# Eight layers on one core: a quarter of one key transpose moved from VectorE to TensorE, reciprocals moved to GpSimd

## The chip, the cores and the metric

The kernel runs on one core of one Trainium2 chip. The metric is device microseconds of one execution, from the first to the last instruction and what lies around it. Before the change three runs gave a median of 3522.67 us (3521.52 to 3526.77).

A core has five engines that run side by side, each with its own queue of instructions: TensorE (PE in the profile, with its weight loads as PEld), VectorE (DVE), ScalarE (ACT), GpSimd (POOL) and SyncE (SP), which starts DMAs here. They wait for one another by semaphores.

## The reference, cut to what matters

A stack of eight layers works on one sequence of 2048 tokens of 128 values, each as `x = x + f(layernorm(x))`: four attentions (L0 to L3) and four feed-forward layers. The attention of L2 is cheap here. Those of L0, L1 and L3 have 16 heads of 64 values and differ in mask and bias:

```python
# L0 (full attention; L1 is causal; L3 has a region mask and a bias per query and head)
Q = jnp.einsum('btd,hkd->bthk', x, W_Q) + b_Q
K = jnp.einsum('btd,hkd->bthk', x, W_K) + b_K
V = jnp.einsum('btd,hkd->bthk', x, W_V) + b_V
scores = jnp.einsum('bqhk,bshk->bhqs', Q, K) / jnp.sqrt(jnp.asarray(d_head, x.dtype))
attn = jax.nn.softmax(scores, axis=-1)
out_h = jnp.einsum('bhqs,bshk->bqhk', attn, V)
return jnp.einsum('bqhk,hdk->bqd', out_h, W_O) + b_O
```

L0 and L3 look at all 2048 keys for every query. The kernel calls these the layers that are not causal; the change calls them full.

## The kernel before, in words

**The order of the work.** Nothing is issued where it is written. Every piece of work is a `Step` (L92) with an engine, an estimated time `us`, a key (tick, place) and lists of steps and buffers that it needs. `run` (L119) is a list scheduler in Python: again and again it takes the engine that can start a step earliest, prefers the lowest key among what is ready, and emits that step's instructions. Each engine then executes its instructions in that order. So the estimates set the order of every queue, though not a single wait. `Ring` and `Held` (L78, L86) are the buffers: a step that takes a buffer waits until the users of the one that it replaces are done.

**One pair, eight groups.** An attention runs pair by pair of heads (8 pairs). `Pair` projects the keys, queries and values of its two heads from the normalised, transposed x: `projected` (L385, eight matmuls of 512 columns a pair), `valued` (L405, four times four matmuls of 128 columns). A `Group` (L420) is 256 queries of a pair, as eight strips of 32 queries. There are 8 groups to a pair, 64 to a layer.

**One group of a full layer**, by step, with its line:

- `score` (L458, matmuls L481): for each of eight strips and both heads, four matmuls of 64x512, one for each quarter of the partitions: the score tile of a strip and a head is 128 x 512. Partition 32c + q holds query q, column 32b + k holds key k of block 4b + c. Two strips are glued to one step, so a group has four. In the profile a 4-byte matmul stands as two records: 32 to such a step. L3 adds a small mask matmul to each strip and head (`picks`).
- `scan` (L491, DVE): copies a score tile from PSUM to the row buffer e and takes its lowest value on the way: 16 a group, each with a short read of the accumulator.
- `spread_lowest` (L525): GpSimd gathers the lowest values (L537), DVE reduces them (L540), in L3 GpSimd adds the bias (L544), ACT hands the result out (L551). Twice a group, for j = 0 and 1, each four strips.
- `exps` (L559, ACT, L563): 16 a group, in place, with their sums.
- `turn` (L577, DVE, L580): transposes 32x32 blocks of e in place, four strips at a time: four a group, (j, h) from (0, 0) to (1, 1), each 128 x 2048. After it, the partitions of 32-column slice t hold keys 128t to 128t + 127.
- `weigh` (L584, matmuls L595): four steps c = 0 to 3 a group, each 8 matmuls (four t, two heads) of 128x256 with v as weights; head 0 writes partitions 0 to 63 of o, head 1 partitions 64 to 127. A step c = 0 waits for all four turns.
- `sum_up` (L607): 8 tiny matmuls (L614) bring the sums to the queries' partitions, DVE takes their reciprocal (L626).
- `project_out` (L631): ACT copies o (L655), PE multiplies by the output weights (L640), ACT scales by the reciprocals (L650), GpSimd adds to x (L668).

A group's scores stand at ticks 4g to 4g + 3, its turns at 4g + 4 to 4g + 7, its weighing at 4g + 8 to 4g + 11 of the pair: three groups are under way at once, with six row buffers e (two a group), four PSUM banks for scores (`BANKS`), three for all else (`MISC`) and one for o.

Of the kernel before, what the change touches and what calls it, by code (L numbers as in the profile page):

```python
# [13 lines left out]
ALU = mybir.AluOpType  # L14
AX = mybir.AxisListType

P = 128
T = 2048
D = 128
NT = T // P  # L20
H = 16
DH = 64
# [8 lines left out]
Q = 32  # L31
NS = 8
# [26 lines left out]
def network(ctx: ExitStack, tc: tile.TileContext, a: dict, out: bass.AP):  # L59
# [128 lines left out]
    MID, MIXED, PAIRED = Ring(work, "mid4", [P, 512], 4), Ring(work, "mid3", [P, 512], 3), Ring(work, "mid2", [P, 512], 2)  # L188
    LOW, SHIFT = Ring(small, "low", [P, 4, NS], 3), Ring(small, "shift", [P, NS], 3)
    SUMS, SHARES = Ring(small, "sums", [P, 2, NS], 3), Ring(small, "r", [P, 2, 2], 3)  # L190
    OUT, PARTS = Ring(small, "oT", [P, NS * Q], 2), Ring(small, "part", [P, 2, D], 4)
    MEANS, NORMED = Ring(small, "mv", [P, 4, 4], 3, ordered=False), Ring(small, "xn", [P, 4, D], 2, ordered=False)

    def keep(shape, name, dtype=F32):
        return one.tile(list(shape), dtype, tag=name, name=name)
# [27 lines left out]
    make_identity(nc, ident)  # L223
    half_power = keep([P, 4], "half_power")
    nc.gpsimd.memset(half_power, -0.5)
    xT = keep([P, PAD + T], "xT")
    nc.gpsimd.memset(xT[:, 0:PAD], 0.0)

# [136 lines left out]
    class Pair:  # L365
# [19 lines left out]
        def projected(self, add, c, to, which, s, takes):  # L385
            pp, b = Held(MISC), self.layer.biases[which]

            def make():
                nc.tensor.matmul(  # L389
                    pp.t, lhsT=self.w.t[:, which, :], rhs=xT[:, cols(4 * c, 4)], start=True, stop=True  # L390
                )

            def copy():
                part = to.t[:, bass.ts(c, 512)] if which else to.t
                if b is not None:
                    nc.scalar.activation(part, pp.t, AF.Identity, bias=b[:, self.p : self.p + 1], scale=s)
                else:
                    nc.scalar.mul(part, pp.t, s)

            uses = [self.w] if takes else [self.w, to]  # L400
            made = add(PE, 0.62, make, self.layer.ready[c], takes=[pp] + takes, uses=uses)
            self.layer.readers[c].append(made)
            return add(ACT, 0.6, copy, uses=[pp, to])

        def valued(self, add, c):  # L405
            pv, v = Held(MISC), self.v[c]

            def make():
                for i in range(4):
                    nc.tensor.matmul(  # L410
                        pv.t[:, bass.ts(i, P)], lhsT=xT[:, cols(4 * c + i)], rhs=self.w.t[:, 2, :], start=True, stop=True
                    )

            made = add(PE, 0.8, make, self.layer.ready[c], takes=[pv, v], uses=[self.w])
            self.layer.readers[c].append(made)
            self.v_made.append(
                add(ACT, 0.6, lambda: nc.scalar.copy(v.t.rearrange("p t d -> p (t d)"), pv.t), uses=[pv, v])
            )

    class Group:  # L420


        def __init__(self, pair, g, t0, late, t1):
            self.pair, self.g, self.layer = pair, g, pair.layer
            self.narrow = self.width(NS - 1) <= 256
            self.rows = [Held(ROWS)] if self.narrow else [Held(ROWS), Held(ROWS)]
            self.sums, self.o, self.oT = Held(SUMS), Held(SUMMED), Held(OUT)
            self.lows, self.shifts = [Held(LOW) for j in range(2)], [Held(SHIFT) for j in range(2)]
            scanned = [self.score(planner(t0 + k, SCORES), planner(t0 + k, LOWEST), k) for k in range(4)]
            turned = []  # L430
            summed = []
            for j in range(2):
                found = scanned[2 * j] + scanned[2 * j + 1]
                shifted = self.spread_lowest(planner(t0 + 2 + 2 * j, SMALL), planner(t0 + 3 + 2 * j, SMALL), j, found)
                for h in range(2):
                    tick = t0 + 4 + 2 * j + h
                    made = [
                        self.exps(planner(tick, MORE if part else EXPS), j, h, part, shifted) for part in range(2)
                    ]
                    summed += made  # L440
                    turned.append(self.turn(planner(tick + late, TURN), j, h, made))
            shares = self.sum_up(planner(t0 + 8, SMALL), summed)
            n = g // 2 + 1 if self.layer.causal else 4
            weighed = []
            for c in range(n):
                weighed = [self.weigh(planner(t1 + c, WEIGH), c, turned + weighed)]
            self.project_out(t1 + n, weighed, shares)
# [10 lines left out]
        def score(self, add, add_scan, k):  # L458
# [37 lines left out]
            needs = pair.k_made[0 : self.g // 2 + 1 if causal else 4] + [pair.q_made[self.g // 2]]  # L496
            needs = needs + masks if causal or masked else needs
            n = self.width(2 * k)
            us = max(0.25, 0.0019 * n) + (0.1 if causal else 0.07 if masked else 0.0)
            used = [pair.kT, pair.qT[self.g // 2]]  # L500
            second = add(PE, us, lambda: make(2 * k + 1, banks[1]), needs, takes=banks[1], uses=used)
            first = add(PE, us, lambda: make(2 * k, banks[0]), needs, takes=banks[0], uses=used, then=second)
# [56 lines left out]
        def exps(self, add, j, h, part, shifted):  # L559
# [14 lines left out]
            us = 2 * (0.29 + 0.00082 * self.width(4 * j))  # L574
            return add(ACT, us, do, [shifted], takes=[self.sums] if first else [], uses=uses)

        def turn(self, add, j, h, made):  # L577
            def do():
                e = self.e(h)[:, bass.ts(j, 4), 0 : self.width(4 * j)]
                nc.vector.transpose(e, e)  # L580

            return add(DVE, 0.06 + 0.00436 * self.width(4 * j), do, made, uses=self.rows)

        def weigh(self, add, c, turned):  # L584

            last = self.width(4) // Q - 1
            ts = range(4 * c, min(4 * c + 4, last + 1))

            def first(t):
                return 4 if t * Q >= self.width(0) else 0  # L590

            def do():
                for t in ts:
                    for h in range(2):
                        nc.tensor.matmul(  # L595
                            self.o.t[bass.ds(DH * h, DH), first(t) : NS, :],
                            lhsT=self.pair.v[c].t[:, t % 4, bass.ds(DH * h, DH)],
                            rhs=self.e(h)[:, first(t) : NS, bass.ts(t, Q)],
                            start=t == 0,
                            stop=t == last,  # L600
                        )

            us = sum(0.27 if first(t) else 0.487 for t in ts)
            uses = self.rows + [self.pair.v[c]] + ([self.o] if c else [])
            return add(PE, us, do, turned + [self.pair.v_made[c]], takes=[] if c else [self.o], uses=uses)

        def sum_up(self, add, made):  # L607

            ps, r = Held(MISC), Held(SHARES)

            def do():
                for j in range(2):
                    for i in range(4):
                        nc.tensor.matmul(  # L614
                            ps.t[bass.ts(i, Q), bass.ts(j, 2)],
                            lhsT=quarters,
                            rhs=self.sums.t[:, :, 4 * j + i],
                            start=True,
                            stop=True,
                        )  # L620

            add(PE, 0.25, do, made, takes=[ps, r], uses=[self.sums])
            self.shared = add(
                DVE,
                0.17,
                lambda: nc.vector.reciprocal(r.t.rearrange("p j h -> p (j h)"), ps.t[:, 0:4]),  # L626
                uses=[ps, r],
            )
            return r

        def project_out(self, tick, weighed, r):  # L631
# [284 lines left out]
    def feed_forward(add, t0, n, after, full, w1T, b1, func, w2T):  # L916

        hT, made, po = [Held(MID) for f in range(NC)], [], Held(MISC)
        for f in range(0, NC, 2):
            ph = [Held(MISC) for k in range(2)]  # L920

            def make(f=f, ph=ph):
                for k in range(2):
                    nc.tensor.matmul(  # L924
                        ph[k].t[:, 0 : P * n],
                        lhsT=w1T()[:, bass.ts(f + k, P)],
                        rhs=xT[:, cols(t0, n)],
                        start=True,
                        stop=True,
                    )  # L930

            def act(k, ph):
                nc.scalar.activation(
                    hT[k].t[:, 0 : P * n], ph.t[:, 0 : P * n], func, bias=b1[:, k : k + 1]
                )

            add(PE, 0.31 * n, make, after, takes=ph + hT[f : f + 2])
            for k in range(2):
                made.append(
                    add(ACT, wide(P * n), lambda k=k, f=f, ph=ph: act(f + k, ph[k]), uses=[ph[k], hT[f + k]])  # L940
                )
# [90 lines left out]
    def rest(add, t0, n, after, hurry, made):  # L1032
# [31 lines left out]
        for to, part, mu in ((xk, rests[1], mu_k), (xr, rests[0], mu_r)):  # L1064
# [4 lines left out]
        edges.append(kept)  # L1069
        add(  # L1070
            PE,
            0.155 * n,
            lambda: nc.tensor.matmul(pk.t[:, 0:m], lhsT=wkk, rhs=xk.t[:, 0:m], start=True, stop=True),
            mixed[0:1],
            takes=[pk, ka],
# [79 lines left out]
    def features(add, c):  # L1155
# [3 lines left out]
        for j in range(3):  # L1159
# [7 lines left out]
            def act(j=j, n=n, ph=ph):  # L1167
                nc.scalar.activation(hm[j].t[0:n, :], ph.t[0:n, :], AF.Gelu, bias=eb1[0:n, j : j + 1])

            add(PE, 0.62, make, L3.ready[c], takes=[ph, hm[j]])  # L1170
            made.append(add(ACT, 0.6 if j else 1.9, act, uses=[ph, hm[j]]))

        def score():
# [204 lines left out]
```

## Time and profile before

| what | before |
|---|---|
| median of three runs | 3522.67 us |
| profiled execution's own time | 3522.59 us |
| its span, first to last instruction | 3520.9 us |
| mean granted TensorE clock | 0.985 |
| PE busy | 3421.9 us (97%) |
| PEld busy | 1722.5 us (49%) |
| DVE busy | 3281.8 us (93%) |
| ACT busy | 2720.9 us (77%) |
| POOL busy | 774.2 us (22%) |
| L0 attention, steady part | about 30 to 1165 us |
| L1 attention, with the layers around it | about 1165 to 2300 us |
| L3 attention, steady part | about 2300 to 3440 us |

Busy time is the union of an engine's instructions. A matmul's end is modelled, so the durations of PE rows overlap; the distance from the start of a step to the start of the next is the firmer number, and it is used below. The chain of waits follows the work that ended last back from the end, each step to what released it. A group of instructions is shown with its count, its busy time, the mean length of one in ns, and the idle time of its engine just before.

### The profile page before, as it was taken

What the parts mean: (1) busy time and instruction counts of PE and PEld (TensorE: products, weight loads), DVE (VectorE), ACT (ScalarE), POOL (GpSimd) and SP (SyncE); (2) the same over time, 40 slices, a digit from 0 to 9 for tenths busy, and PEclk for the clock granted to TensorE, in tenths of its full rate; (3) what the DMA queues carried; (4) which work ended last, traced back from release to release, by engine and by line L of the source; (5) the groups of instructions that cost most, each with busy time, mean ns of one, the idle gap of its engine ahead of it and who ended that gap; (6) DMA issues with size and microseconds to landing.
All of it is one profiled execution on the core that took longest, in us unless ns stands there. A gap on an engine that the chain in (4) does not pass through costs nothing.

```text
span 3520.9 us, 111995 instructions
## 1 busy us (share of the span) xinstructions
PE 3421.9 (97%) x45482; PEld 1722.5 (49%) x45482; DVE 3281.8 (93%) x8147; ACT 2720.9 (77%) x8451; POOL 774.2 (22%) x2452
## 2 busy tenths in 40 slices
PE   8999999999999999999999988899999999999998
PEld 3444444444444354555566655444444444444445
DVE  8999999999999988999999883699999999999996
ACT  6778777778777667888888974577777777777786
POOL 2111111111111243223323353221111111111122
PEclk9999999999999999999999998899999999999999
DMA  1000000000000000000000000000000000000000
GB/s 47 2 5 2 5 5 2 5 2 5 2 5 5 1 5 8 6 6 6 6 6 6 6 2 4 4 5 5 2 5 2 5 5 2 5 2 2 2 5 10
DMA packets 22944, 18.76 MB, mean 5 GB/s; under 512 B 3556, under 2 KB 21612, under 8 KB 22426
## 3 DMA queue, kind: packets, MB, share of 16 engines
q1 hardware_dynamic: 22362, 11.55, 1.2%
q8 instruction: 356, 5.83, 0.7%
q14 instruction: 162, 1.33, 0.1%
q0 software_dynamic: 64, 0.06, 0.0%
HBM read 10.60 MB, written 1.05 MB: 3 GB/s over the span
## 4 chain that ended last, share of the span: by engine, by line
DVE 57%; PE 36%; issue 5%; ACT 1%; POOL 1%; DMA 0%; SPq 0%; POOLq 0%; DVEq 0%; ACTq 0%
DVE e L491 31%; DVE e L580 23%; PE s L481 13%; PE o L595 12%; PE t L389 3%; PE t L410 2%; PE t L640 1%; PE t L882 1%; PE t L946 1%; PE t L924 1%; DVE shift L540 1%; DVE st L240 1%; PE t L614 1%; DVE mv L241 0%; PE t L1197 0%
## 5 line engine op out<-in xcount | busy, mean ns | idle before, releaser
L563 ACT ACTIVATE e<-e,shift 128x512 f32<-128x512 f32 (+15 forms) x3072 | 1972.7, 649 | 33.4 <-POOL shift L551 24.7
L491 DVE TENSOR_SCALAR_CACHE_REDUCE e<-s 128x512 f32<-128x512 f32 (+15 forms) x3072 | 1656.8, 587 | 55.1 <-PE s L481 53.1
L481 PE MATMUL s<-kT,qT 64*32 64x512 f32 (+8 forms) x24576 | 1513.1, 534 | 25.6 <-DVE e L491 25.5
L580 DVE STREAM_TRANSPOSE e<-e 128x2048 f32<-128x2048 f32 (+10 forms) x768 | 1503.9, 1959 | 6.7 <-ACT e L563 6.6
L595 PE MATMUL o<-e,v 128*64 128x256 f32 (+1 forms) x10496 | 1310.8, 385 | 16.9 <-DVE e L580 16.7
L595 PEld LDWEIGHTS o<-e,v 128*64 128x64 f32 x10496 | 723.8, 137 | 622.0 <-issue 283.1
L481 PEld LDWEIGHTS s<-kT,qT 64*32 64x32 f32 x24576 | 429.2, 105 | 584.3 <-DVE e L491 346.6
L563 ACT ACTIVATION_READ_ACCUMULATOR e<-e,shift 128x1 f32 x3072 | 595.3, 194 | 0.0
L537 POOL COPY low<-low 32x8 f32<-32x8 f32 x1152 | 209.1, 182 | 1265.2 <-DVE e L491 1217.8
L551 ACT COPY shift<-shift 32x8 f32<-32x8 f32 x768 | 149.9, 195 | 377.2 <-POOL shift L545 200.4
L668 POOL TENSOR_TENSOR x<-x,part 128x256 f32<-128x256 f32 x384 | 280.7, 731 | 623.8 <-ACT part L650 608.3
L650 ACT ACTIVATE part<-t,r 128x128 f32<-128x128 f32 x768 | 217.5, 364 | 45.2 <-PE t L640 43.1
L491 DVE DVE_READ_ACCUMULATOR e<-s 128x1 f32 x3072 | 228.2, 74 | 0.0
L389 PE MATMUL t<-xT,w 128*128 128x512 f32 x384 | 216.2, 649 | 3.1 <-ACT xT L276 3.1
L481 PE MATMUL s<-beyond,eye 64*32 64x32 bf16 x2560 | 159.3, 176 | 0.0
L655 ACT COPY oT<-o 128x256 f32<-128x256 f32 x192 | 71.1, 370 | 109.4 <-PE o L595 109.1
L640 PEld LDWEIGHTS t<-w,oT 64*128 64x128 f32 x1536 | 101.8, 186 | 91.3 <-issue 35.2
L640 PE MATMUL t<-w,oT 64*128 64x128 f32 x1536 | 139.2, 298 | 1.5 <-ACT oT L655 1.2
L481 PEld LDWEIGHTS <-regions 64*32 64x32 bf16 x1024 | 73.1, 93 | 137.6 <-issue 108.2
L544 POOL TENSOR_TENSOR shift<-shift,bias 32x8 f32<-32x8 f32 x128 | 25.0, 195 | 442.0 <-DVE shift L540 442.0
L481 PE MATMUL s<-picks,regions 64*32 64x8 bf16 x1024 | 121.3, 166 | 0.0
L481 PEld LDWEIGHTS <-eye 64*32 64x32 bf16 x2560 | 97.9, 93 | 43.3 <-issue 20.8
(178 smaller groups left out, 1591.9 us busy)
## 6 DMA issues: line engine op xcount, KB each, us to landing
w<-in_L_wq SPq DMA_DIRECT2D x24, 64.0 KB, 2.0
w<-in_L_wk SPq DMA_DIRECT2D x24, 64.0 KB, 2.2
w<-in_L_wv SPq DMA_DIRECT2D x24, 64.0 KB, 2.1
w<-in_L_wo SPq DMA_DIRECT2D x24, 64.0 KB, 2.0
x<-in_x SPq DMA_DIRECT2D x4, 256.0 KB, 4.2
out_x<-x SPq DMA_DIRECT2D x3, 256.0 KB, 2.3
big<-in_L_wo SPq DMA_DIRECT2D x1, 512.0 KB
big<-in_moe_w SPq DMA_DIRECT2D x1, 512.0 KB
```

The lines of the kernel that those rows point to most:

```text
L389: nc.tensor.matmul(pp.t, lhsT=self.w.t[:, which, :], rhs=xT[:, cols(4 * c, 4)], start=True, stop=True)
L481: nc.tensor.matmul(s[h].t[on, bass.ds(first, size)], lhsT=lhsT, rhs=rhs, start=m == 0, stop=m == len(terms) - 1,)
L491: nc.vector.tensor_scalar(self.e(h)[:, i, 0:n], s.t[:, 0:n], 1.0, None, ALU.mult, ALU.min, accum_out=self.lows[j].t[:, 0, 4 * h + i % 4 : ...
L537: nc.gpsimd.tensor_copy(low.t[0:Q, c], low.t[bass.ts(c, Q), 0])
L551: (nc.gpsimd.tensor_copy if causal else nc.scalar.copy)(shift.t[bass.ts(c, Q)], first())
L563: nc.scalar.activation(e, e, AF.Exp, bias=self.shifts[j].t[:, 4 * h + i % 4 : 4 * h + i % 4 + 1], scale=-1.0, accum_out=self.sums.t[:, h, ...
L580: nc.vector.transpose(e, e)
L595: nc.tensor.matmul(self.o.t[bass.ds(DH * h, DH), first(t) : NS, :], lhsT=self.pair.v[c].t[:, t % 4, bass.ds(DH * h, DH)], rhs=self.e(h)[:, ...
L640: nc.tensor.matmul(y[h].t[:, bass.ts(j, P)], lhsT=oT.t[half, bass.ts(j, P)], rhs=pair.w.t[half, 3, :], start=True, stop=True,)
L650: nc.scalar.mul(part.t[:, j, :], y[h].t[:, bass.ts(j, P)], r.t[:, j, h : h + 1])
L655: lambda: nc.scalar.copy(oT.t, self.o.t.rearrange("p i q -> p (i q)")),
L668: POOL, 0.74, lambda part=part: nc.gpsimd.tensor_tensor(xs, xs, part.t, ALU.add), [divided], uses=[part]
```

## The change

In the full layers, of the turn (j, h) = (1, 1) only the first three quarters, 384 of the 512 columns of its four strips, stay on DVE. The last 128 columns of each of these four strips are transposed by TensorE (four matmuls against the identity into a MISC bank), and ACT copies them back into e. A whole 128x128 transpose leaves the keys in another order than the transpose of 32x32 blocks does. So GpSimd makes, once a pair, a second copy `va` of the last quarter of v for head 1, with its keys in that order (16 small copies), and in the weigh step c = 3 the four matmuls of head 1 are split into two of 128 columns each: strips 0 to 3 with v, strips 4 to 7 with `va`.

In the full layers the reciprocals move as well: ACT copies the four sums from PSUM, and GpSimd raises them to the power -1.

The ring `PARTS` has 3 buffers instead of 4. The estimates `us` of several PE steps are changed: projections 0.62 to 1.0, scores from max(0.25, 0.0019 n) to max(0.2, 0.06 + 0.00168 n), weighing from 0.487 a t to 0.435 with 0.08 a step, and those of some matmuls in the feed-forward layers.

```diff
-    OUT, PARTS = Ring(small, "oT", [P, NS * Q], 2), Ring(small, "part", [P, 2, D], 4)
+    OUT, PARTS = Ring(small, "oT", [P, NS * Q], 2), Ring(small, "part", [P, 2, D], 3)
+    APART = Ring(work, "va", [P, 4, DH], 2)
...
+    inverse = keep([P, 4], "inverse")
+    nc.gpsimd.memset(inverse, -1.0)
...
-            made = add(PE, 0.62, make, self.layer.ready[c], takes=[pp] + takes, uses=uses)
+            made = add(PE, 1.0, make, self.layer.ready[c], takes=[pp] + takes, uses=uses)
...
+            if c == 3 and not self.layer.causal:
+                self.va = Held(APART)
+
+                def regroup(i):
+                    for q in range(4):
+                        nc.gpsimd.tensor_copy(self.va.t[bass.ts(i, Q), q, :], v.t[bass.ts(q, Q), i, DH:P])
+
+                self.va_made = [
+                    add(
+                        POOL, 1.0, lambda i=i: regroup(i), self.v_made[3:],
+                        takes=[] if i else [self.va], uses=[v, self.va] if i else [v],
+                    )
+                    for i in range(4)
+                ]
...
-                    turned.append(self.turn(planner(tick + late, TURN), j, h, made))
+                    turned += self.turn(planner(tick + late, TURN), j, h, made)
...
-            us = max(0.25, 0.0019 * n) + (0.1 if causal else 0.07 if masked else 0.0)
+            us = max(0.2, 0.06 + 0.00168 * n) + (0.1 if causal else 0.07 if masked else 0.0)
...
+        def apart(self, j, h):
+
+            return j == h == 1 and not self.layer.causal
+
         def turn(self, add, j, h, made):
+
+
+            n = self.width(4 * j) - (P if self.apart(j, h) else 0)
+
+            def rows():
+                return self.e(h)[:, bass.ts(j, 4), :]
+
             def do():
-                e = self.e(h)[:, bass.ts(j, 4), 0 : self.width(4 * j)]
-                nc.vector.transpose(e, e)
-
-            return add(DVE, 0.06 + 0.00436 * self.width(4 * j), do, made, uses=self.rows)
+                nc.vector.transpose(rows()[:, :, 0:n], rows()[:, :, 0:n])
+
+            turned = [add(DVE, 0.06 + 0.00436 * n, do, made, uses=self.rows)]
+            if self.apart(j, h):
+                pt = Held(MISC)
+
+                def turn_apart():
+                    for i in range(4):
+                        nc.tensor.transpose(pt.t[:, bass.ts(i, P)], rows()[:, i, n : n + P], ident)
+
+                def copy():
+                    nc.scalar.copy(rows()[:, :, n : n + P], pt.t.rearrange("p (i n) -> p i n", i=4))
+
+                add(PE, 0.75, turn_apart, made, takes=[pt], uses=self.rows)
+                turned.append(add(ACT, 0.6, copy, uses=[pt] + self.rows))
+            return turned
...
+                        parts = [(first(t), NS, self.pair.v[c].t[:, t % 4, bass.ds(DH * h, DH)])]
+                        if c == 3 and self.apart(1, h):
+                            parts = [(0, 4, parts[0][2]), (4, NS, self.pair.va.t[:, t % 4, :])]
+                        for i0, i1, lhsT in parts:
+                            nc.tensor.matmul(
+                                self.o.t[bass.ds(DH * h, DH), i0:i1, :],
+                                lhsT=lhsT,
+                                rhs=self.e(h)[:, i0:i1, bass.ts(t, Q)],
+                                start=t == 0,
+                                stop=t == last and i1 == NS,
+                            )
+
+            us = 0.08 + sum(0.24 if first(t) else 0.435 for t in ts)
...
+            def invert():
+                some = r.t.rearrange("p j h -> p (j h)")
+                nc.gpsimd.tensor_tensor(some, some, inverse, ALU.pow)
+
+            copied = add(
+                ACT, 0.17, lambda: nc.scalar.copy(r.t.rearrange("p j h -> p (j h)"), ps.t[:, 0:4]), uses=[ps, r]
+            )
+            self.shared = add(POOL, 1.05, invert, [copied], uses=[r])
...
-            add(PE, 0.31 * n, make, after, takes=ph + hT[f : f + 2])
+            add(PE, 0.45 * n, make, after, takes=ph + hT[f : f + 2])
...
-            0.155 * n,
+            0.24 * n,
...
-            add(PE, 0.62, make, L3.ready[c], takes=[ph, hm[j]])
+            add(PE, 1.0, make, L3.ready[c], takes=[ph, hm[j]])
```

In the causal layer L1 turns, weighing and reciprocals stay as they were; its steps have the new estimates.

More of the change, by code (lines that the diff above doesn't have):

```diff
@@ L594, in do @@
                     for h in range(2):
[L595 to L605, printed above, removed]
+                        parts = [(first(t), NS, self.pair.v[c].t[:, t % 4, bass.ds(DH * h, DH)])]
[10 more added lines that the diff above has]
+            us = 0.08 + sum(0.24 if first(t) else 0.435 for t in ts)
+            uses, made = self.rows + [self.pair.v[c]] + ([self.o] if c else []), [self.pair.v_made[c]]
+            if c == 3 and self.apart(1, 1):
+                uses, made = uses + [self.pair.va], made + self.pair.va_made
+            return add(PE, us, do, turned + made, takes=[] if c else [self.o], uses=uses)
         def sum_up(self, add, made):
@@ L622, in sum_up @@
             add(PE, 0.25, do, made, takes=[ps, r], uses=[self.sums])
[L623 to L627, printed above, removed]
+            if self.layer.causal:
+                self.shared = add(
+                    DVE,
+                    0.17,
+                    lambda: nc.vector.reciprocal(r.t.rearrange("p j h -> p (j h)"), ps.t[:, 0:4]),
+                    uses=[ps, r],
+                )
+                return r
+            def invert():
[3 more added lines that the diff above has]
+                ACT, 0.17, lambda: nc.scalar.copy(r.t.rearrange("p j h -> p (j h)"), ps.t[:, 0:4]), uses=[ps, r]
             )
+            self.shared = add(POOL, 1.05, invert, [copied], uses=[r])
             return r
```

## The prediction

> **What bounds the kernel now.** First the page's busy shares and its chain of waits:
>
> ```profile
> PE 3421.9 (97%) x45482; PEld 1722.5 (49%) x45482; DVE 3281.8 (93%) x8147; ACT 2720.9 (77%) x8451; POOL 774.2 (22%) x2452
> ...
> DVE 57%; PE 36%; issue 5%; ACT 1%; POOL 1%; DMA 0%; SPq 0%; POOLq 0%; DVEq 0%; ACTq 0%
> ```
>
> PE looks fullest, yet the chain runs mostly through DVE. So the windows by stage (L0 steady, L1, the passage from L1 to L3, L3 steady; columns PE, PEld, DVE, ACT, POOL):
>
> ```profile
> 101.00:1133.00 1032.00, 1027.14 (x12172) 458.27 (x12168) 1030.16 (x2132) 813.57 (x2425) 139.60 (x437) 1.00 0.01 4
> ...
> 1305.00:2016.00 711.00, 701.96 (x13575) 420.27 (x13580) 652.47 (x2336) 604.42 (x2242) 231.25 (x840) 1.00 0.03 7
> 2016.00:2320.00 304.00, 266.64 (x2537) 153.95 (x2522) 200.61 (x594) 191.31 (x493) 104.89 (x229) 0.88 0.02 4
> 2320.00:3400.00 1080.00, 1075.06 (x13522) 517.96 (x13521) 1076.58 (x2236) 841.89 (x2518) 193.39 (x685) 1.00 0.01 3
> ```
>
> In the full layers DVE has no idle time (99.7 to 99.8%); in L1 it has (92%), and PE is the fuller. How full PE really is in L0 is read from starts in its timeline:
>
> ```profile
> 643.28 1.95 PE L481 MATMUL s<-kT,qT 64*32 64x512 f32 x32
> 645.16 1.12 PE L389 MATMUL t<-xT,w 128*128 128x512 f32 x2
> 646.21 2.06 PE L595 MATMUL o<-e,v 128*64 128x256 f32 x16
> ...
> 668.02 1.95 PE L481 MATMUL s<-kT,qT 64*32 64x512 f32 x32
> 669.90 1.95 PE L595 MATMUL o<-e,v 128*64 128x256 f32 x16
> 671.77 1.95 PE L481 MATMUL s<-kT,qT 64*32 64x512 f32 x32
> ```
>
> A score step that waits for nobody takes 669.90 - 668.02 = 1.88 us, a weigh step 671.77 - 669.90 = 1.87, a projection 1.05. Likewise (same timeline) L410 takes 1.09, L614 0.24, L640 0.65. Where PE comes early, a score step is stretched to 2.5 or 2.8 us by waiting for banks: busy, but slack.
>
> **Floors of one group**, each engine by itself. DVE: 16 scans 9.66 (four take 2.41 to 2.42 in its timeline), four turns of 2.23, two L540 0.22, reciprocal 0.09: 18.89. Measured: the oT copies (L655) from 227.8 to 1133.4 us are 48 periods, 18.87. DVE is the bound. PE in L0: 4 x 1.88 + 4 x 1.88 + 0.24 + 0.65 + projections (8 x 1.06 + 4 x 1.09)/8 = 1.60, sum 17.53. In L3 a score step has masks:
>
> ```profile
> 2623.16 1.10 PE L481 MATMUL s<-kT,qT 64*32 64x512 f32 x16
> 2624.05 0.17 PE L481 MATMUL s<-picks,regions 64*32 64x8 bf16 x1
> ...
> 2625.21 0.72 PE L640 MATMUL t<-w,oT 64*128 64x128 f32 x8
> ```
>
> 2.05 instead of 1.88: floor 17.53 + 4 x 0.17 = 18.21. L3's period is 18.98 from 2446.6 to 2750.2 and 18.89 from 2910.0 to 3363.4, mean 18.93; the pair between takes 159.8 instead of 151.8, the 8 us of DVE work that prepares the last layer's weights. So PE has 1.34 us a group to spare in L0, 0.7 in L3.
>
> **What the Trainium skill says.** "Trainium Kernel Development and Optimization", Performance Expectations: matmul busy time is a bad metric, since matmuls are pipelined. Agreed: 99.5% busy beside a floor of 17.53 in 18.87 (93%). "TensorEngine Tiling (Array Packing)", Key Properties: changing the tiling mode drains the engine. Agreed: L614, 16 records of two columns, holds PE for 0.24. "TensorE: Matmul & The Clock Gate", Part 4: a transpose of a full 128x128 lands in PSUM and needs a copy; the change pays one, on ACT. The same page, Part 3, says matmuls are strict FIFO. Here the trace differs: the mask matmul is issued third, after two records of the first quarter, and starts after 16 records (above). Matmuls on other parts of the array pass a waiting one.
>
> **The change, part by part.** Rows for its prices:
>
> ```profile
> L580 DVE STREAM_TRANSPOSE e<-e 128x2048 f32<-128x2048 f32 x528 | 1210.2, 2292 | 4.8 <-ACT e L563 4.8
> ...
> L417 ACT COPY v<-t 128x512 f32<-128x512 f32 x96 | 55.8, 581 | 51.4 <-PE t L410 51.4
> ...
> L580 DVE STREAM_TRANSPOSE e<-e 128x1536 f32<-128x1536 f32 x16 | 28.1, 1758 | 0.0
> ...
> L246 POOL TENSOR_TENSOR mv<-mv,half_power 128x4 f32<-128x4 f32 x27 | 28.2, 1045 | 2.3
> ```
>
> - DVE, on the path: one turn of 128x1536, the shape that L1 has: 2292 - 1758 = 0.53 less; reciprocal 0.09 less. New floor 18.87 - 0.62 = 18.25 in both layers. L540 stays.
> - PE, four transposes: L261 does the same shape, 4 at 1314.96, next step at 1315.55: 0.59, drains included. Bounds 0.53 (no drain of its own beside a projection) and 0.75.
> - PE, split weighing: columns stay equal (head 1 streams 2 x 128 beside head 0's 256), 8 more records a group on head 1's half. Bounds: 0, and 0.87 if the second half runs alone (4 t x 2 records x 0.109, half of the 0.216 between record pairs of a 256-column step, 1.73/8). Less than nothing is excluded: no column is saved and records are added. I take 0.03, since parts of the array queue separately. New PE floors: L0 18.15, L3 18.83.
> - ACT: copy 0.58 and copy of sums about 0.2 (L551's 195 ns): 0.8 a group on 14.9 (813.57 x 18.87/1032), so 15.7 of 18.4. What queues behind the copy's wait for PE are the next exps, then turns. In the timeline the last exps of a group end at 599.7 and their turn starts at 606.21: 6.5 us of cover. The copy also gates weigh c = 0, which before waited for the turn ending 608.4; free too. Without cover they cost their length, 0.78 x 120 = 94 us.
> - PE's new wait for the exps: behind it stand the next score and weigh; L614 already waits for the same exps, so nothing new while it stands beside it.
> - POOL: power 1.05 a group, 16 copies a pair (0.18 to 0.45 each, L537's 182 ns being smaller; I take 0.3: 4.8). Queued behind are the gathers L537: one ends 606.97, its reader L540 starts 610.95: 4 us of cover. The power is needed by L650, 8 us after L614. `va` is first read four ticks (18 us) after v. No DMA moves.
> - PARTS: a buffer is held from L640 (607.33) to L668's end (610.44), 3 us a period; three suffice. The new MISC use holds a bank about 2 us.
> - Estimates: they reorder queues in L1 and the two passages. L1 is PE-bound and keeps its work; the passages (1133 to 1305, 2016 to 2320) have 15 and 37 us of idle PE. I take 0, bounds -10 and +10.
>
> **Sum.** What comes next is PE: in L0 it stands 0.10 under DVE's floor, in L3 0.58 over it. Two engines so equal, coupled by four banks, wait for each other now and then. L3 before (floors 18.21 and 18.87) lost 0.06. For L0 I take 0.15, bounds 0 and 0.4: 18.40, gain 0.47 x 60 steady groups = 28. L3: 18.83 + 0.05 = 18.88, gain 0.05 x 60 = 3, and DVE's new slack there (0.63 x 8 = 5) covers 5 of the 8 us of weight work. Together 36: 3522.6 of the profiled execution (span 3520.9 and 1.7 around it) becomes 3487; the median, 3522.67, is the same within 0.1.
>
> **Rivals.** (1) Full relief: L0 at 18.25, transposes at 0.53 and no losses in L3 (18.80): 37 + 8 + 8 = 53, 3470. For it: DVE lost nothing in L0 before. Chance 0.16. (2) Coupling costs more: L0 18.6 (16), L3 19.0 (-4), weight work 5: 3506. For it: misc PE work falls unevenly on ticks. Chance 0.18. (3) Slower: the split's second half runs with nothing beside it, 0.87 a group on PE: L0 19.04 (+10), L3 19.72 (+47), less 8: 3572. It decides from about 0.4 us of additional PE time a group, where L0's gain and L3's loss are even. For it: the skill's FIFO; against it: the passing seen above. Chance 0.10. (4) The reordered passages eat the gain: no change, 0.06. The likeliest, 3475 to 3499: 0.50.
>
> Faster by over 0.2% (7 us, about what a measurement here can tell from no change): 0.50 + 0.16 + 0.18 = 0.84; same 0.06; slower 0.10. The range 3460 to 3512 takes in cases 1 and 2 with the passages' spread.
>
> **What would show it.** L0 periods of 18.4 with DVE idle under 1%; L3 periods of 18.9 with DVE about 97% busy, its scans waiting for PE scores; transposes of 0.55 to 0.6 from start to start; c = 3 weigh steps of 1.9. A c = 3 step over 2.3, or L3 periods over 19.1, would make the prediction wrong; so would turns waiting for ACT.

## The result, and the profile after

The changed kernel takes 3493.5 us (median of four runs, 3491.93 to 3494.54), the kernel before in the same comparison 3524.3 us: ratio 0.9909, 95% interval 0.9897 to 0.9922, a small gain but clear of the spread (the lowest of the four runs before is 3521.52). The forecast was 3487, range 3460 to 3512. The profiled execution took 3494.28 us with a span of 3492.6, 28.3 us under the span before.

Busy shares of the page, and the windows by stage cut at the same places of the work (L0 steady, L1, passage from L1 to L3, L3 steady; columns PE, PEld, DVE, ACT, POOL):

```profile
PE 3397.9 (97%) x47018; PEld 1844.2 (53%) x47018; DVE 3211.9 (92%) x8019; ACT 2807.6 (80%) x8709; POOL 965.4 (28%) x2837
```

```profile
101.00:1107.00 1006.00, 1006.00 (x12778) 509.67 (x12771) 994.63 (x2064) 848.06 (x2526) 219.41 (x601) 1.00 0.01 4
1290.00:1998.00 708.00, 698.14 (x13358) 415.31 (x13356) 644.79 (x2300) 597.97 (x2214) 227.62 (x827) 1.00 0.02 7
1998.00:2300.00 302.00, 259.35 (x2490) 153.07 (x2478) 195.45 (x583) 193.93 (x502) 111.56 (x247) 0.88 0.01 4
2300.00:3380.00 1080.00, 1079.27 (x14465) 576.07 (x14466) 1061.93 (x2222) 893.28 (x2665) 279.75 (x868) 1.00 0.01 3
```

PE shows hardly any idle time in either full layer, which alone says nothing, since steps that wait for banks count as busy. DVE tells the two apart. In L3 it is idle 1.7% of the time, nearly all of it waiting for PE's scores: there the bound has moved from DVE to PE. In L0 its 1.1% of idle time lies mostly in the first pair, and four steady pairs have 3.2 us of it: there DVE is still the bound. The waits of DVE in these four pairs (374.5 to 963.3 us), then in L3 (2300 to 3380 us):

```profile
DVE e L508 <- PE s L498: 3.2, 4, 0.8
```

```profile
DVE e L508 <- PE s L498: 16.3, 34, 1.2
DVE shift L557 <- POOL low L554: 0.3, 1, 0.3
```

The shapes that the change makes, from the groups in the same stretch of L0 (count, busy us, mean ns):

```profile
L607 DVE STREAM_TRANSPOSE e<-e 128x2048 f32<-128x2048 f32 x96 | 220.0, 2292 | 0.0
...
L607 DVE STREAM_TRANSPOSE e<-e 128x1536 f32<-128x1536 f32 x32 | 56.3, 1761 | 0.0
...
L680 POOL TENSOR_TENSOR r<-r,inverse 128x4 f32<-128x4 f32 x32 | 32.6, 1019 | 74.5 <-ACT r L683 74.2
...
L618 ACT COPY e<-t 128x512 f32<-128x512 f32 x32 | 18.6, 582 | 0.8 <-PE t L615 0.8
...
L427 POOL COPY va<-v 32x64 f32<-32x64 f32 x64 | 14.8, 231 | 44.0 <-ACT v L420 41.3
```

And one stretch of PE's timeline with a split weigh step, a projection and the four transposes:

```profile
703.57 0.65 PE L639 MATMUL o<-e,v 128*64 128x256 f32 x4
703.85 0.38 PE L639 MATMUL o<-e,va 128*64 128x128 f32 x2
...
705.47 1.12 PE L392 MATMUL t<-xT,w 128*128 128x512 f32 x2
706.43 0.60 PE L615 MATMUL t<-ident,e 128*128 128x128 f32 x4
706.96 1.95 PE L498 MATMUL s<-kT,qT 64*32 64x512 f32 x32
```

From start to start: the split step 705.47 - 703.57 = 1.90 us, the transposes 0.53, and the projection beside them 0.96, where before it took 1.06 between steps of other shapes.

Where the time went is best read from the start of each group's oT copy, one for each of the 192 groups (L655 before, L712 after). How far the changed kernel is ahead at such a mark:

| mark | before, us | after, us | ahead, us |
|---|---|---|---|
| first group of L0 | 72.9 | 74.7 | -1.8 |
| last but three of L0 | 1228.1 | 1200.4 | 27.8 |
| ninth of L1 | 1461.7 | 1437.5 | 24.2 |
| 57th of L1 | 2009.9 | 1998.1 | 11.9 |
| first of L3 | 2293.0 | 2288.0 | 5.0 |
| last of L3 | 3504.6 | 3477.7 | 26.8 |
| end | 3520.9 | 3492.6 | 28.3 |

L0 gave 28 to 30 us, as forecast. L1 and the passages, forecast at nothing, took 23 of them back: 3.6 up to the ninth group of L1, 5.2 in its second pair (100.8 us instead of 95.6), 7.1 in the next five and 6.9 from there to L3. L3, forecast at 8, gave 22. A steady pair took 147.2 us in L0 (151.1 before), 96.4 in L1 (95.1), 149.6 in L3 (151.8).

### The profile page after: what moved, and what is told of

Same layout as the page of the kernel before. It is cut to its first block, busy times and chain, and to the rows that moved or that the text cites. A ratio compares the mean times of both kernels' runs of the same rounds, so it can differ in the third digit from the quotient of the medians.

```text
span 3492.6 us, 115619 instructions
## 1 busy us (share of the span) xinstructions
PE 3397.9 (97%) x47018; PEld 1844.2 (53%) x47018; DVE 3211.9 (92%) x8019; ACT 2807.6 (80%) x8709; POOL 965.4 (28%) x2837
## 5 line engine op out<-in xcount | busy, mean ns | idle before, releaser
L580 ACT ACTIVATE e<-e,shift 128x512 f32<-128x512 f32 (+14 forms) x3072 | 1973.9, 648 | 28.2 <-POOL shift L568 20.1
L498 PE MATMUL s<-kT,qT 64*32 64x512 f32 (+8 forms) x24576 | 1458.4, 534 | 22.3 <-DVE e L508 22.3
L607 DVE STREAM_TRANSPOSE e<-e 128x2048 f32<-128x2048 f32 (+10 forms) x768 | 1435.2, 1871 | 9.3 <-ACT e L580 8.9
L639 PE MATMUL o<-e,v 128*64 128x256 f32 (+1 forms) x10496 | 1270.2, 374 | 6.1 <-DVE e L607 4.3
L639 PEld LDWEIGHTS o<-e,v 128*64 128x64 f32 x10496 | 748.3, 137 | 545.3 <-issue 297.7
L498 PEld LDWEIGHTS s<-kT,qT 64*32 64x32 f32 x24576 | 416.5, 105 | 518.8 <-issue 215.9
L680 POOL TENSOR_TENSOR r<-r,inverse 128x4 f32<-128x4 f32 x128 | 130.5, 1020 | 304.4 <-ACT r L683 303.7
L712 ACT COPY oT<-o 128x256 f32<-128x256 f32 x192 | 70.7, 368 | 162.2 <-PE o L639 162.1
L639 PE MATMUL o<-e,va 128*64 128x128 f32 x1024 | 195.5, 273 | 0.0
L697 PE MATMUL t<-w,oT 64*128 64x128 f32 x1536 | 139.8, 299 | 0.5 <-ACT xT L279 0.3
L697 PEld LDWEIGHTS t<-w,oT 64*128 64x128 f32 x1536 | 102.3, 187 | 67.9 <-issue 24.6
L639 PEld LDWEIGHTS o<-e,va 128*64 128x64 f32 x1024 | 126.0, 137 | 0.0
L498 PEld LDWEIGHTS <-regions 64*32 64x32 bf16 x1024 | 65.6, 93 | 113.4 <-issue 79.4
```

Of the source, the lines that this page charges most:

```text
L498: nc.tensor.matmul(s[h].t[on, bass.ds(first, size)], lhsT=lhsT, rhs=rhs, start=m == 0, stop=m == len(terms) - 1,)
L580: nc.scalar.activation(e, e, AF.Exp, bias=self.shifts[j].t[:, 4 * h + i % 4 : 4 * h + i % 4 + 1], scale=-1.0, accum_out=self.sums.t[:, h, ...
L607: nc.vector.transpose(rows()[:, :, 0:n], rows()[:, :, 0:n])
L639: nc.tensor.matmul(self.o.t[bass.ds(DH * h, DH), i0:i1, :], lhsT=lhsT, rhs=self.e(h)[:, i0:i1, bass.ts(t, Q)], start=t == 0, stop=t == las ...
L680: nc.gpsimd.tensor_tensor(some, some, inverse, ALU.pow)
L697: nc.tensor.matmul(y[h].t[:, bass.ts(j, P)], lhsT=oT.t[half, bass.ts(j, P)], rhs=pair.w.t[half, 3, :], start=True, stop=True,)
```

## The experiments

**What was open.** Theory A: the new estimates reorder the queues of L1 and the passages and cost the 23 us. Rivals: PARTS with three buffers does it; or the added work holds up the passages. And the price of the split, which decided the slower rival, was to be measured by itself.

### All estimates old, on the changed kernel

```diff
-            made = add(PE, 1.0, make, ...
+            made = add(PE, 0.62, make, ...
-            us = max(0.2, 0.06 + 0.00168 * n) + ...
+            us = max(0.25, 0.0019 * n) + ...
-            us = 0.08 + sum(0.24 if first(t) else 0.435 for t in ts)
+            us = sum(0.27 if first(t) else 0.487 for t in ts)
```

and the three of the feed-forward and feature matmuls.

> The changed kernel with all six PE estimates as they were before; the three new parts and the PARTS ring of 3 stay. Marks in the traces (start of every group's oT copy) show that the changed kernel leads by 28 us at the end of L0, by only 5 us when L3 starts, and by 27 at the end of L3; a steady pair of L1 takes 96.4 us instead of 95.1. Theory A, the new estimates reorder L1 and the two passages and lose the 23 us: L1 pair back at 95.1, lead at the start of L3 20 to 28, total 3470 to 3480. Rival B, PARTS with 3 buffers is what reorders L1: pair stays at 96.4, total 3490 to 3496. Rival C, the added work itself (a MISC bank, ACT copies) holds up the passages: lead still falls there by 9 + 10 us, total 3485 to 3493.

Measured: 3505.53 us, ratio to before 0.9942 (0.9927 to 0.9957), 12 us slower than the changed kernel: no theory's number. The marks say why. L1 pairs are back at 95.1, and from the end of L0 to the end of L1 the lead falls by 1.3 us, where the changed kernel lost 16: there A holds. From the 57th group of L1 to the first of L3 it falls by another 5.0 (6.9 in the changed kernel): there A does not hold. And the first pair of L0 takes 171.3 us instead of 152.6, steady L0 pairs 147.8 instead of 147.2. In that first pair PE's longest wait (138 to 175 us) is one that the change made:

```profile
PE t L615 <- ACT r L683: 5.6, 1, 5.6
```

The transposes wait for a MISC bank that the tiny sums hold until ACT has copied them; in the changed kernel's order no such wait of this size occurs. DVE then stands for 8.8 us. Over the whole first pair PE stands 8.7 us longer than in the changed kernel, and its mean granted clock is 0.94 instead of 0.98, by an estimate from these figures another 7 us (0.06 x 171.3 less 0.02 x 152.6). So the new estimates do two things: they cost in L1, and they save the start of L0 in this kernel.

### The new estimates alone, on the kernel before

> The kernel before with the six new estimates and nothing else. Theory A: L1 pair 96.4 instead of 95.1, the passages longer, total 3535 to 3548. Rivals B and C: 3521 to 3528, L1 pair 95.1.

Measured: 3543.98 us, ratio 1.0051 (1.0036 to 1.0066), that is slower. L1 pairs take 95.7, the pair at the passage from L0 to L1 164.6 instead of 152.4, and the marks fall behind by 22.7 us between the end of L0's seventh pair and the end of L1, nothing else having changed. The total is the one that A named. A's number for the steady pair (96.4) is not: the estimates alone make 0.6 of the 1.3 us.

### PARTS of three alone, on the kernel before

```diff
-    OUT, PARTS = Ring(small, "oT", [P, NS * Q], 2), Ring(small, "part", [P, 2, D], 4)
+    OUT, PARTS = Ring(small, "oT", [P, NS * Q], 2), Ring(small, "part", [P, 2, D], 3)
```

> The kernel before with PARTS of 3 buffers and nothing else. Theory A: within 5 us of before, L1 pair 95.1. Rival B: L1 pair 96.4, total 3532 to 3548.

Measured: 3531.47 us (19 executions, 3527.83 to 3537.62), ratio 1.0015 (1.0008 to 1.0022). That is 4.8 us over the kernel before, within A's 5, and L1 pairs stay at 95.1. The two profiled executions lie further apart, 3533.58 and 3522.59 us. In their traces all pairs are as before but the two at the passage from L0 to L1: 179.8 instead of 175.9 and 159.2 instead of 152.4, 11 us by the marks.

Order cannot be the whole of these 11 us. In the first of the two pairs PE, DVE, ACT and POOL have the same instructions in the same order in both traces (the first difference comes at 1315.6 us of before), and where ACT waits before it writes a `part` buffer, it never waits for the GpSimd addition that frees one. Still the pair is 3.9 us longer, PE is busy 5.2 us longer, and PE's granted clock (the third number from the end; before, then with PARTS of 3) is lower:

```profile
1133.40:1309.30 175.90, 160.88 (x1800) 75.95 (x1802) 156.39 (x456) 119.47 (x388) 57.96 (x134) 0.96 0.01 2
1133.80:1313.60 179.80, 166.07 (x1799) 77.74 (x1802) 155.87 (x456) 119.42 (x388) 57.98 (x134) 0.92 0.01 2
```

In the second pair the clock is 0.96 instead of 0.99. Executions of one and the same kernel differ in this way too: in this comparison those of the kernel before with a mean clock of 0.985 or 0.986 have spans of 3519.3 to 3520.7 us, those with 0.983 spans of 3523.9 to 3527.3. At 0.983 the kernel with PARTS of 3 has 3529.4 to 3529.8. So PARTS is a second cause, on this kernel in one place and worth a few us; the rest of the 11 goes with the clock, and no run here shows what lowered it. A difference of a few us in a passage between two traces is therefore not yet a difference of order.

### The split weigh step undone

```diff
-                        if c == 3 and self.apart(1, h):
+                        if False:
                             parts = [(0, 4, parts[0][2]), (4, NS, self.pair.va.t[:, t % 4, :])]
```

> The changed kernel with head 1 of the weigh step c = 3 as one matmul of 256 columns with v for all strips; it leaves out the second order of keys for strips 4 to 7, the columns streamed and all else stay. If the split costs 0.03 us a group or nothing, as predicted: within 3 us of the changed kernel, 3490 to 3496. If the second half runs alone, as the slower rival had it (0.87 a group): 40 to 60 us faster, nearly all in L3.

Measured: 3491.28 us, ratio 0.99 (0.9886 to 0.9915), 2 us from the changed kernel. Steady pairs: L0 147.2 in both, L3 149.5 against 149.6. The split is free, and the slower rival falls. DVE, ACT and POOL have the same order here as in the changed kernel, so this run also shows how far a passage moves without it: from the 61st group of L0 to the ninth of L1 234.2 us at a clock of 0.98, in the changed kernel 237.1 at 0.96. The 2.9 us between them are most of the 3.6 that the changed kernel loses there.

### The causal layer with its old estimates, the full layers with the new

```diff
+            us = 0.62 if self.layer.causal else 1.0
...
-            us = max(0.2, 0.06 + 0.00168 * n) + ...
+            us = (max(0.25, 0.0019 * n) if causal else max(0.2, 0.06 + 0.00168 * n)) + ...
...
+            if self.layer.causal:
+                us = sum(0.27 if first(t) else 0.487 for t in ts)
```

> The changed kernel, but the causal layer's scores, weighing and projections keep their old estimates; the full layers have the new ones. In the changed kernel's queue a steady L1 pair has two score steps in a row twice, in the kernel before once; a score step takes all four banks, so the second waits for DVE's scans. Theory A: L1 pairs at 95.1 again (1.3 each less), the region from the end of L0 to the last L1 group 10 to 20 us shorter than in the changed kernel, total 3474 to 3485. Rival: the order costs nothing and something in the added work does: pairs stay 96.4, total 3490 to 3496.

Measured: 3489.82 us, ratio 0.9897 (0.9881 to 0.9914). L1 pairs are at 95.1, so the order is the cause there. But the pair at the passage takes 163.5 instead of 147.7, and at the 57th group of L1 the lead is 11.7 us, no better than the changed kernel's 11.9; the total misses the expected 3474 to 3485.

What the order does in L1 is seen in PE's timeline of a steady pair. Before, two score steps of one group stand next to each other, then a weigh step, then the next score step:

```profile
1659.40 0.90 PE L481 MATMUL s<-kT,qT 64*32 64x384 f32 x16
...
1663.21 1.95 PE L595 MATMUL o<-e,v 128*64 128x256 f32 x16
1665.09 0.53 PE L481 MATMUL s<-kT,qT 64*32 64x160 f32 x16
...
1666.06 0.31 PE L614 MATMUL t<-sums,quarters 128*32 128x2 f32 x16
```

After, the third score step comes ahead of the weigh step:

```profile
1642.21 0.90 PE L498 MATMUL s<-kT,qT 64*32 64x384 f32 x16
...
1645.98 0.33 PE L498 MATMUL s<-kT,qT 64*32 64x160 f32 x4
...
1647.68 1.95 PE L639 MATMUL o<-e,v 128*64 128x256 f32 x16
```

The same step of 160 columns takes 1666.06 - 1665.09 = 0.97 us behind the weigh step and 1647.68 - 1645.98 = 1.70 without it: its four banks come free only as DVE scans them, and nothing else stands in PE's queue meanwhile. Over three steady pairs all of PE's other steps take the same time in both kernels; the score steps take 133.2 us instead of 129.1, and that is the 1.3 to 1.4 us a pair. A steady pair of the changed kernel has two such places. PE's order of steps in the fifth and sixth pairs of L1 is the same in the kernel before and in this run (95.1), and again the same in the changed kernel and in the run without the transposes below (96.4, both with new estimates and PARTS of 3). With the new estimates and PARTS of 4 it has only the first of the two places (95.7, on the kernel before and on the changed one). So the new estimates move one score step ahead, and with them the ring of three moves a second, at about 0.7 us each.

### The same, with PARTS of four

```diff
-    ... Ring(small, "part", [P, 2, D], 3)
-    APART = Ring(work, "va", [P, 4, DH], 2)
+    ... Ring(small, "part", [P, 2, D], 4)
+    APART = Ring(work, "va", [P, 4, DH], 1)
```

> As hybrid, and PARTS has its 4 buffers again (APART has 1 instead of 2, for room). With 3 buffers alone on the kernel before, the passage from L0 to L1 was 11 us longer. Theory A: that is a want of buffers, and comes back: total 8 to 12 us under hybrid. Rival: it is an accident of another order: within 5 us of hybrid, either way.

Measured: 3473.39 us, ratio 0.9856 (0.9841 to 0.987): 16 us under the run above, more than theory A's 8 to 12 and the rival's 5, and faster than both kernels. The lead at the marks is 28.6 us near the end of L0, 28.2 at the end of L1, 27.1 at the first group of L3, 49.0 at its last. L1 and the passages cost 1.5 us in all. Steady pairs of the full layers are those of the changed kernel (147.2 and 149.6): the whole difference of 20 us between these two kernels lies in L1 and the passages. In the passage from L0 to L1 (from the 61st group of L0 to the ninth of L1, 233.3 us against 251.0 in the run above) PE's scores wait less for DVE's scans; above, then here:

```profile
PE s L499 <- DVE e L509: 9.9, 10, 2.7
PE s L499 <- DVE e L509: 3.4, 4, 1.6
```

The granted clock there is 0.98 instead of 0.95, by an estimate from these figures about 8 us (0.05 x 251.0 less 0.02 x 233.3). A want of buffers is not seen as a wait: in neither trace does ACT, before it writes `part`, wait for GpSimd. The stages of this run, L0 and L1:

```profile
101.00:1106.00 1005.00, 1005.00 (x12787) 508.90 (x12795) 995.22 (x2069) 848.28 (x2527) 218.46 (x601) 1.00 0.01 4
1284.00:1982.00 698.00, 691.78 (x13374) 414.45 (x13378) 643.71 (x2298) 597.66 (x2216) 227.50 (x827) 1.00 0.02 7
```

Beside the changed kernel's second row (708 us for the same 56 groups, ACT, DVE and POOL equal within 0.2%) it is the same work in 10 us less.

### The reciprocals back on DVE

```diff
-            if self.layer.causal:
+            if True:
                 self.shared = add(
                     DVE,
```

> The changed kernel with the reciprocals of the full layers on DVE, as before. Prediction's working: DVE's floor in L0 rises by 0.09 a group, 0.7 a pair (147.9), nothing in L3, where PE bounds: total 3496 to 3502. Rival: in L0 the engines' mutual waits bound, not DVE's floor: pair 147.2, total 3491 to 3496.

Measured: 3532.63 us, ratio 1.002 (1.0011 to 1.0028): both expectations far off. Steady pairs: 149.0 in L0 (+1.8), 150.8 in L3 (+1.2); and L1 and the passages cost 28 us. In L0's steady part DVE is busy 588.53 us for 32 groups instead of 585.56, which is the 0.09 a group of the prediction. The rest is idle time, 7.6 us instead of 3.2, most of it in a wait that the changed kernel does not have:

```profile
DVE shift L557 <- POOL low L554: 6.5, 4, 1.6
DVE e L508 <- PE s L498: 1.1, 4, 0.3
```

Once a pair the reduction stands in DVE's queue too early for its gather. That is order again, and not a wait of the reciprocal for PE, which has no row here. In L3 nothing was expected and 0.15 a group was found; which part of that is order was not followed.

### Without the transposes on TensorE

```diff
-            return j == h == 1 and not self.layer.causal
+            return False
...
-            if c == 3 and not self.layer.causal:
+            if False:
```

> The changed kernel without the transposes on TensorE and the second copy of v: new estimates, PARTS of 3, reciprocals on GpSimd stay. Against the run with the new estimates alone (3544): DVE 0.09 a group less, 0.7 a pair in L0 and in L3: 3528 to 3538. If the reciprocals alone carried the gain: under 3515.

Measured: 3525.65 us, ratio 1.0004 (0.9996 to 1.0013), 18 us under the new estimates alone and below the expected 3528; that run has PARTS of 4, so the two differ in the ring as well. Steady L0 pairs take 150.6 against 151.6, L3 pairs 151.2 against 151.1, so here the reciprocals are worth 1.0 us a pair in L0 and nothing in L3. In the traces, 12.6 us apart, the whole difference is there by the last groups of L0, whose first pairs and last groups differ as well.

With the new estimates and PARTS of 3 neither part alone beats the kernel before. Steady pairs of L0 and L3 take 151.1 and 151.8 us before, 150.6 and 151.2 with the reciprocals alone, 149.0 and 150.8 with the transposes alone, 147.2 and 149.6 with both. The transposes bring most of the gain; what the reciprocals add in L0, 1.0 or 1.8, depends on what stands beside them.

### PARTS of four with all new estimates, and with all old

> The changed kernel, estimates all new, with PARTS of 4 and APART of 1. If each cause costs in its own place: steady pairs of L0 147.2, of L1 96.4 (the estimates' order), of L3 149.6 as in the changed kernel; the passages move by up to 15 us either way; total 3478 to 3495. If PARTS of 3 was the whole loss of L1: L1 pairs 95.1, total 3470 to 3478.

Measured: 3494.63 us, ratio 0.9915 (0.99 to 0.993), no gain. L1 pairs take 95.7, neither theory's 96.4 nor 95.1, since PARTS moves a step in L1 as well; the passage from L0 to L1 gains 4 us (232.9 instead of 237.1) and the second pair of L1 loses 6 (107.1 instead of 100.8).

> The run with all old estimates on the changed kernel, with PARTS of 4 and APART of 1. That run lost 22 us in L0's first pair, where PARTS is little used. If the first pair's loss comes from the estimates: it stays (first pair 168 to 173), total 3495 to 3507. If it came with the three PARTS: first pair 151 to 155, total 3475 to 3488.

Measured: 3509.28 us, ratio 0.995 (0.9934 to 0.9967). L0's first pair stays at 171.0, so its loss belongs to the old estimates; the total is 2 us over the expected 3507.

## Why the prediction was right, point by point

**DVE in L0, held.** The turn of 128x1536 was taken at 1758 ns and measures 1761. Floor 18.25 a group, loss 0.15, period 18.40; measured 147.2/8 = 18.40, with DVE busy 18.30 (585.56/32) and idle 0.10, 0.6% where under 1% was named.

**PE's additions, a little dear.** Transposes 0.59: measured 0.54 a group. Split 0.03: measured 0.02 (weighing 7.54 a group in L0, 7.51 with the split undone). The reading behind it, that matmuls on other parts of the array pass a waiting one, fits the split step's 1.90 us. That L614 holds PE for 0.24 us does not by itself show a drain, since it has 16 records to run; the clearer sign of a price for changing the shape is the projection, 0.96 us ahead of the transposes and 1.06 ahead of scores.

**L3, the size was off.** The term said: floor 18.83, period 18.88, 3 us in 60 groups. Measured 149.6/8 = 18.70. The floor itself was too high: transposes and value projections now often stand beside a query or key projection of the same shape, and those take 0.97 a group instead of 1.06, and the four transposes 0.54 instead of 0.59. From start to start, waits included, a group has 8.23 of scores, 7.55 of weighing, 0.54 of transposes, 0.97 and 0.53 of projections, 0.24 and 0.65 for L660 and L697, 18.70 before rounding; the scores are only 0.03 over 4 x 2.05, so PE hardly waits. The gain is 0.23 x 60 = 14 us instead of 3. The weight work was right: its pair costs 2.8 us more than the others instead of 8.0, 5 us as forecast.

**The estimates, the step that failed.** "I take 0, bounds -10 and +10", and "L1 is PE-bound and keeps its work". The work was kept and the time was not: between the last groups of L0 and the first of L3 the lead fell by 22.8 us. The misses of L3 (14 us more than forecast) and of L1 with the passages (23 less) partly cancel: 36 forecast; measured 28 + 22 - 23 + 1.5 at the end = 28. That the total came nearer than its parts is luck. The argument that a PE-bound stage cannot lose by reordering overlooked that PE's own queue can put two steps that want the same four banks in a row. That both causes, estimates and ring, act through order is shown for the steady L1 pairs by PE's order of steps and the timeline. In the passages it is shown only that the two edits together undo the loss (the version with both costs 1.5 us there). There the granted clock moves as well, by some us even where the order is the same, and no run holds it fixed.

**Cover, held.** ACT's copy and the POOL steps stay out of the way: turns wait for ACT 8.9 us in the whole run (6.6 before), and no weigh step in L0's steady part waits for the copy. The one bank wait of 5.6 us showed only with the old estimates.

**Rivals.** Full relief came true in L3 (18.80 named, 18.70 measured) but not in L0. The slower one is refuted. The fourth, passages that eat the gain, was given 0.06 for no change at all; its mechanism took 23 us, though the gain stayed.

What stays open: how the loss in the passages divides between waits and the granted clock, and what lowers the clock there; why the passage from L1 to L3 is longer with all estimates new and with all old, but hardly with the mixture; how much of L3's rise with the reciprocals on DVE is order, and which of the estimates moves L1's score step ahead.

## What to carry to other kernels

Find each engine's floor from start-to-start times in a steady stretch; the period after a move from one engine to another came out here within 1% of the higher of the new floors. Where a list scheduler writes the queues, any change of an estimate or a ring is a change of the whole program: compare marks along the run beside the totals, with the granted clock of each stretch, and price reordering at what the waits of other orders show. Try the move with the estimates and buffers of the untouched stages left as they were before judging it: here that was worth 20 us, two thirds of the gain of 31. It is no rule: leaving all the estimates as they were, those of the full layers too, cost 12 to 16 us.

## What the runs showed that was not expected

- Two steps side by side that both use the array whole (128*128 in the rows) save PE about 0.1 us: a projection takes 0.96 before the transposes and 1.06 before scores; 0.08 us a group in L0 and L3 came from such neighbours.
- Matmuls of 128 columns on one half of the array, two for each of 256 columns on the other, cost 1.90 us a step instead of 1.88.
- With the same order of instructions, one stretch of about 176 us took 3.9 us more at a granted clock of 0.92 than at 0.96.
- Reordering alone, by edits that change no instruction, moved this kernel from 3526.67 to 3543.98 us (estimates), and the changed one from 3493.5 to 3473.39.
